# Six chunks of a fused 1x1 product by seven half-depth products instead of eight, in two gated layers, and a new order of small work in the last layer

## The chip, the cores and the metric

The kernel runs on one core of one Trainium2 chip. The metric is device time in microseconds (us). The engines are TensorE (PE, with its weight loads as PEld), VectorE (DVE), ScalarE (ACT), GpSimd (POOL) and SyncE (SP). SP and ACT also issue DMA transfers from their queues, and each engine works through a list of instructions of its own.

## The reference

Four layers act on one map of 512 channels and 64x64 pixels, each as `x = x + layer(group_norm(x))`, all in float32. Layer 0 is attention and isn't touched by the change. Layers 1 and 2 are the gated layers, and layer 3 is a linear attention:

```python
# layers 1 and 2: DIMS = [128, 256, 512]
fused = conv1x1(x, w_in, b_in)              # 512 -> 1024 channels
pwa, abc = fused[:, :128], fused[:, 128:]   # abc: 896 channels = 7 chunks of 128
dw_abc = dwconv7(abc, dw_w, dw_b)           # depthwise, 7x7
h = pwa * dw_abc[:, :128]
h = conv1x1(h, pw0_w, pw0_b) * dw_abc[:, 128:384]
h = conv1x1(h, pw1_w, pw1_b) * dw_abc[:, 384:]
return conv1x1(h, w_out, b_out)
...
# layer 3: 768 channels = 6 chunks
qkv0 = affine_nchw(conv2d(x, w_qkv), s_qkv, b_qkv)
agg = affine_nchw(conv2d(qkv0, w_dw, groups=768, pad=2), s_dw, b_dw)
...
```

## The kernel before

X stays on chip as 4 channel chunks of 128 partitions by 4096 pixels, cut into 8 blocks of 512 pixels. A "product" below is one matmul of a 128x128 weight with a 128x512 block. It is float32, and the profile shows each such product as two matmul records.

**Gated layers** (`_gated_convs`, twice). For each of the seven convolved chunks i and each block k, `fused(i, k)` makes four products (one for each input chunk) into one PSUM bank, and DVE moves the bank with the bias added into a plane buffer (L965). A DMA on ACT's queue then writes the plane to DRAM (tensor F[i], L720). There are two plane buffers, one for even and one for odd blocks. When all eight blocks of chunk i are there, `_PlaneConv.conv` does the depthwise convolution of the chunk as small matmuls: SP's queue loads the taps T (L729) and shifted rows S (L745), ACT copies S once more (L752), TensorE runs 8 parts of 96 records each into PSUM (`ps_cv`), DVE transposes the result (L806, and at the end four larger ones, L812), and ACT adds the bias (L1024).

Work of TensorE that needs no convolution is laid between the parts. `convolve(i, first, between)` issues the list `first` ahead of the first part and deals the list `between` out over the parts, by number of entries. The lists hold fused inputs, gates (`gate(i, b)`: products of earlier results, then a DVE multiply, L987) and outputs (`output`, products with `w_out`, then DVE additions into X, L999 and L1003). The order of TensorE's instructions is the program's. Those of DVE, ACT and the queues are laid out by a scheduler when the program is built. All products but the convolution's share four PSUM banks (pool `ps_mm`). Five weight buffers (`w2p`) and five large buffers (`hp`, one for each convolution result) rotate.

**Layer 3** (`_linear_attention`) already makes its fused product by `_Seven`: for a pair of weight chunks (a, b) and a pair of pixel blocks, with the depth of 512 halved, seven half-depth products (p1 to p7, two matmuls each) take the place of eight. It needs sums of the weights (`sums`, L844), differences of the blocks (`differences`, L858), two kept copies of PSUM banks made by ACT (L1225), two DVE additions to them (L891, L895), and four moves into planes (`put`: L1167 on ACT, L1172 and L1175 on DVE). Its weights are multiplied by `s_qkv` on POOL (L1125) and by the group norm's factor on ACT or DVE (`_Centered.scaled`, L363 and L366). `prepare(hf, q)` loads rows of k back and makes k positive (L1102), with its sums (L1335), ahead of the steps of a block.

The convolution and fill lists of the gated layers before the change are:

```python
b0, b12, b34, b56 = (inputs(c) for c in ((0,), (1, 2), (3, 4), (5, 6)))
...
convolve(0, b12[:6], b12[6:])
convolve(1, g[0][:3], g[0][3:] + b34[:6])
convolve(2, [], b34[6:])
convolve(3, b56[:4], b56[4:8] + g[1] + g[2])
convolve(4, [], b56[8:])
```

Of the kernel before, what the change touches and what calls it, by code (L numbers as in the profile page):

```python
# [127 lines left out]
def trunk_kernel(ctx: ExitStack, tc: tile.TileContext, a: dict, out: bass.AP):  # L128
# [42 lines left out]
    def new_stats():  # L171
# [11 lines left out]

    stats = _attention(tc, a, X, ident, gmask, neg2, small, new_stats, centered)

    late = ctx.enter_context(tc.tile_pool(name="late", bufs=1))
    s_qkv = late.tile([P, NQKV, P], FP, tag="s_qkv", name="s_qkv")
    nc.gpsimd.dma_start(
        out=s_qkv.rearrange("p i m -> p (i m)"),
        in_=bass.AP(a["L3_s"].tensor, a["L3_s"].offset, [[0, P], [1, NQKV * P]]),  # L190
    )
    stats = _gated_convs(tc, a, X, vcol, gmask, small, new_stats, centered, stats, F)
    _linear_attention(tc, a, X, vcol, vall, ident, gmask, small, centered, stats, F3, Z, s_qkv, out)


def _attention_general(tc, a, X, O, ident, neg2):
# [469 lines left out]
class _PlaneConv:  # L666
# [36 lines left out]
    def take(self, i, k, ps, fill):  # L703
# [18 lines left out]
            in_=t.rearrange("p n r w -> p n (r w)"),  # L722
        )

    def load(self, i, hf, wT, r):
        nc, f = self.nc, self.f
        nl = self.nl
# [96 lines left out]
class _Seven:  # L824
# [35 lines left out]
    def steps(self, a, b, s, t, x, bank, keep, put):  # L860

        nc = self.nc
        ps, kept = {}, {}

        def add(j, w, hs, first):

            if first:
                ps[j] = bank(j)  # L870
            for c in range(2):
                self.matmul(
                    ps[j], w[:, c], hs[c], start=(first and c == 0), stop=(c == 1),
                    skip_group_check=not first,
                )

        def p1():
            add(0, a[:, 0:2], [x(c, 0) for c in range(2)], True)
            kept[0] = keep(0, ps[0])

        def p5():
            add(1, s[0], t[0], True)
            kept[1] = keep(1, ps[1])

        def p2():
            add(0, a[:, 2:4], [x(2 + c, 0) for c in range(2)], False)
            put(0, 0, ps[0], None)

        def p7():
            add(2, s[2], t[2], True)  # L890
            nc.vector.tensor_add(kept[1], kept[1], ps[2])  # L891

        def p6():
            add(3, s[1], t[1], True)
            nc.vector.tensor_add(kept[0], kept[0], ps[3])  # L895

        def p3():
            add(1, s[3], [x(2 + c, 1) for c in range(2)], False)
            put(0, 1, ps[1], kept[0])
            put(1, 1, kept[1], kept[0])  # L900

        def p4():
            add(2, b[:, 2:4], t[3], False)
            put(1, 0, ps[2], kept[0])

        return [p1, p5, p2, p7, p6, p3, p4]


@with_exitstack
def _gated_convs(ctx, tc, a, X, vcol, gmask, small, new_stats, centered, stats, F):  # L910

# [2 lines left out]
    wp = ctx.enter_context(tc.tile_pool(name="cw", bufs=1))  # L916
    w2p = ctx.enter_context(tc.tile_pool(name="cw2", bufs=5))
    hp = ctx.enter_context(tc.tile_pool(name="ch", bufs=5))
    ps_mm = ctx.enter_context(tc.tile_pool(name="ps_mm", bufs=4, space=PSUM))
    ps_cv = ctx.enter_context(tc.tile_pool(name="ps_cv", bufs=4, space=PSUM))  # L920
    pc = _PlaneConv(ctx, tc, FORM, F, ps_cv, NL, 4, False)

    for layer in ("L1", "L2"):
# [24 lines left out]
        def product(w, hs):  # L948
# [2 lines left out]
                pc.matmul(ps, w(c), h, start=(c == 0), stop=(c == len(hs) - 1))  # L951
            return ps

        def taking(w, k):

            return product(lambda c: w[:, c, :], [pc.pixels(X[:, c, :], k) for c in range(NC)])

        def fused(i, k):
# [7 lines left out]
                    dst, src, vcol(pre + "b_in", 1 + i), None, ALU.add  # L966
                ),
            )
            if k == NB - 1 and len(w_in) < NDW:
                w_in.append(centered.scaled(weights("w_in", 1 + len(w_in)), rstd, nc.scalar))  # L970

        D = {}

        def gate(i, b):

# [13 lines left out]
        def output(chunks, b, o):  # L989
# [14 lines left out]
            if chunks[-1] == NDW - 1:  # L1004
                nc.vector.bn_stats(stats[:, o, b, :], xs)

        def blocks(f, i):
            return [lambda b=b: f(i, b) for b in range(NB)]

        def inputs(chunks):  # L1010
            return [lambda i=i, b=b: fused(i, b) for b in range(NB) for i in chunks]

        def outputs(*chunks):
            return [lambda b=b, o=o: output(chunks, b, o) for b in range(NB) for o in range(NC)]

        w_out = []

        def convolve(i, first, between):
# [6 lines left out]

            taps = a[f"{layer}_T"]
            pc.ahead(i, 0, taps)
            for f in first:
                f()

            parts = FORM.nr // FORM.run
            late = min(len(between) // 12, 2)
            early = len(between) - 3 * late
            done = 0
            for part, _ in enumerate(pc.conv(i, 0, taps, bias, D[i], True)):
                if part < parts:
                    upto = early * (part + 1) // parts
                else:
                    upto = done + late
                for f in between[done:upto]:  # L1040
                    f()
                done = upto

        b0, b12, b34, b56 = (inputs(c) for c in ((0,), (1, 2), (3, 4), (5, 6)))
        g = [blocks(gate, i) for i in range(NDW)]
        for f in b0:
            f()
        convolve(0, b12[:6], b12[6:])
        convolve(1, g[0][:3], g[0][3:] + b34[:6])
        convolve(2, [], b34[6:])  # L1050
        convolve(3, b56[:4], b56[4:8] + g[1] + g[2])
        convolve(4, [], b56[8:])
        convolve(5, g[3], outputs(3))
        convolve(6, [], g[4] + outputs(4))
        for f in g[5] + g[6] + outputs(5, 6):
            f()
    return stats


@with_exitstack  # L1060
def _linear_attention(ctx, tc, a, X, vcol, vall, ident, gmask, small, centered, stats, F, Z, s_qkv, out):

# [7 lines left out]
    vcs = 1.0 / N  # L1072

    lq = ctx.enter_context(tc.tile_pool(name="lq", bufs=1))
    w_proj = lq.tile([P, NC, C], FP, tag="w_proj", name="w_proj")
    nc.scalar.dma_start(out=w_proj, in_=a["L3_w_proj"])
    ksum = small.tile([P, NC, NB], FP, tag="ksum", name="ksum")
# [33 lines left out]
    with ExitStack() as st:  # L1111
# [8 lines left out]
        def weights(i):  # L1120
# [1 line left out]
                "p (c n) -> p c n", c=NC  # L1122
            )
            nc.sync.dma_start(out=t, in_=a["L3_w_qkv"][i])
            nc.gpsimd.tensor_tensor(  # L1125
                t, t, s_qkv[:, i].unsqueeze(1).to_broadcast([P, NC, P]), ALU.mult
            )
            return t

        w_qkv = [weights(i) for i in range(4)]  # L1130

# [21 lines left out]
            return ps  # L1153

        for i, w in enumerate(w_qkv):
            centered.scaled(w, rstd, nc.scalar if i else nc.vector)
        centered.began()

        def taken(k):
# [2 lines left out]

        def put(i, k, ps, more=None):

            if more is None:
                bias = vcol(pre + "b_qkv", i)
                pc.take(i, k, [ps], lambda d, x: nc.scalar.activation(d, x, AF.Identity, bias=bias))  # L1167
                return

            def fill(d, x, y):  # L1170
                if i % 2 == 0 or k % 2:
                    nc.vector.tensor_add(d, x, y)  # L1172
                    return
                for n in range(pc.pair):
                    nc.vector.scalar_tensor_tensor(  # L1175
                        d[:, n], x[:, n], step_b[:, i // 2 : i // 2 + 1], y[:, n],
                        ALU.add, ALU.add,
                    )

            pc.take(i, k, [ps, more], fill)  # L1180

        def fused(i, k):
            w = w_qkv[i]
# [71 lines left out]

        def more_weights():
            for i in (4, 5):
                w_qkv.append(centered.scaled(weights(i), rstd, nc.scalar))

        dve, pool = nc.vector, nc.gpsimd  # L1260
        made = [
# [159 lines left out]
        def steps(hf, q):  # L1421
# [7 lines left out]
            [  # L1429
                both(added, *early[:1]),  # L1430
                both(*early[1:4]),
                both(*early[4:7]),
                both(*early[7:10], prepare(0, 0)),
                both(*early[10:13]),
                both(*early[13:]),
            ],
# [200 lines left out]
```

## Time and profile before

| | |
|---|---|
| median of three runs | 3932.12 us (3929.24 to 3934.1) |
| the profiled execution's own time | 3927.94 us |
| its span in the trace | 3926.1 us |
| mean granted TensorE clock | 0.995 |
| matmul records on PE | 35622 |
| attention | to about 2290 us |
| layer 1 | about 2294 to 2801 us |
| layer 2 | about 2801 to 3307 us |
| layer 3 | about 3307 us to the end |

The profile lists each group of instructions with its line, engine, operation, the tile it writes and the tiles it reads, the shape, the number of instructions, then the busy time and the mean duration in ns, then the idle time of the engine ahead of the group and what ended it. Its windows give the busy time of each engine in a stretch of the span, its timelines give the instructions in order of time.

### The profile page before, as it was taken

What the parts mean: (1) busy time and instruction counts of PE and PEld (TensorE: products, weight loads), DVE (VectorE), ACT (ScalarE), POOL (GpSimd) and SP (SyncE); (2) the same over time, 40 slices, a digit from 0 to 9 for tenths busy, and PEclk for the clock granted to TensorE, in tenths of its full rate; (3) what the DMA queues carried; (4) which work ended last, traced back from release to release, by engine and by line L of the source; (5) the groups of instructions that cost most, each with busy time, mean ns of one, the idle gap of its engine ahead of it and who ended that gap; (6) DMA issues with size and microseconds to landing.
All of it is one profiled execution on the core that took longest, in us unless ns stands there. A gap on an engine that the chain in (4) does not pass through costs nothing. (4 is left out here: it accounts for less than half of the span.)

```text
span 3926.1 us, 81449 instructions
## 1 busy us (share of the span) xinstructions
PE 3847.3 (98%) x35622; PEld 1714.3 (44%) x35622; DVE 2370.2 (60%) x2607; ACT 1976.8 (50%) x2857; POOL 119.3 (3%) x101
## 2 busy tenths in 40 slices
PE   6999999999999999999999989999999999999999
PEld 4533335333354333453333335554455544455544
DVE  3577763777736777637767733466534576675435
ACT  3577762777726777536656644452244532354210
POOL 0000000000000000000000000000000000121110
PEclk9999999999999999999999999999999999999999
DMA  2000000000000000000000035552155520463334
GB/s 97 9 1 1 1 1 9 1 1 1 1 1 9 1 1 2 1 9 1 1 1 1 1 113 160 181 167 69 51 155 178 165 79 34 139 185 99 93 92 141
DMA packets 193943, 221.52 MB, mean 56 GB/s; under 512 B 13400, under 2 KB 138584, under 8 KB 193456
## 3 DMA queue, kind: packets, MB, share of 16 engines
q1 hardware_dynamic: 166832, 157.12, 14.3%
q10 hardware_dynamic: 26640, 58.72, 4.0%
q8 instruction: 281, 4.60, 0.5%
q14 instruction: 78, 0.64, 0.1%
q0 software_dynamic: 112, 0.45, 0.0%
HBM read 156.46 MB, written 59.77 MB: 55 GB/s over the span
## 5 line engine op out<-in xcount | busy, mean ns | idle before, releaser
L516 ACT ACTIVATE pt<-ps_s,A 128x512 f32<-128x512 f32 x2048 | 1286.2, 687 | 554.8 <-PE ps_s L508 527.0
L599 DVE TENSOR_TENSOR acc<-acc,pt 128x1024 f32<-128x1024 f32 x960 | 1175.6, 1225 | 331.7 <-ACT pt L516 306.1
L526 PE MATMUL av<-pt,V 64*64 64x512 f32 x8192 | 1112.5, 590 | 0.9 <-ACT pt L516 0.9
L508 PE MATMUL ps_s<-O,K 64*64 64x512 f32 x8192 | 1111.5, 589 | 0.0
L526 PEld LDWEIGHTS av<-pt,V 64*64 64x64 f32 x8192 | 339.7, 133 | 557.2 <-issue 525.4
L508 PEld LDWEIGHTS ps_s<-O,K 64*64 64x64 f32 x8192 | 334.3, 133 | 553.7 <-issue 308.6
L752 ACT COPY S<-S 32x1295 f32<-32x1295 f32 (+1 forms) x272 | 341.1, 1256 | 286.0 <-DMA S<-F 169.7
L693 PE MATMUL ps<-X,w_in_L 128*128 128x512 f32 x896 | 404.7, 604 | 5.2 <-DMA w_in_L<-in_L_w_in_dram 2.8
L965 DVE TENSOR_SCALAR plane<-ps,vec 128x512 f32<-128x512 f32 x112 | 83.7, 748 | 293.8 <-PE ps L693 245.8
L693 PEld LDWEIGHTS ps<-X,w_in_L 128*128 128x128 f32 x896 | 166.5, 191 | 204.0 <-issue 194.5
L693 PEld LDWEIGHTS ps_cv<-S,T 64*32 64x32 f32 x13824 | 194.0, 106 | 109.3 <-issue 73.7
L693 PE MATMUL ps_cv<-S,T 64*32 64x128 f32 x13824 | 231.5, 273 | 4.8 <-DVE turned L806 2.2
L463 PE MATMUL ps_qk<-X,wqkv 128*128 128x512 f32 x512 | 228.3, 599 | 2.8 <-ACT wqkv L363 2.8
L693 PE MATMUL ps<-h,w_out_L 128*128 128x512 f32 x512 | 228.4, 599 | 0.5 <-DVE X L999 0.5
L355 ACT ACTIVATE X<-X,gn_less 128x512 f32<-128x512 f32 x120 | 76.9, 710 | 218.1 <-DVE gn_less L102 206.1
L467 ACT ACTIVATE O<-ps_qk 128x512 f32<-128x512 f32 x32 | 19.1, 596 | 259.2 <-PE ps_qk L463 259.2
L1024 ACT ACTIVATE h<-h,vec 128x1024 f32<-128x1024 f32 x56 | 63.7, 1148 | 167.2 <-DVE h L812 167.0
L463 PEld LDWEIGHTS ps_qk<-X,wqkv 128*128 128x128 f32 x512 | 95.9, 192 | 114.3 <-issue 110.9
L693 PEld LDWEIGHTS ps<-h,w_out_L 128*128 128x128 f32 x512 | 94.3, 190 | 116.7 <-issue 100.5
L987 DVE SCALAR_TENSOR_TENSOR h<-ps,vec,h 128x512 f32<-128x512 f32 x112 | 82.5, 742 | 103.0 <-PE ps L693 97.5
L693 PE MATMUL ps<-h,pw_L 128*128 128x512 f32 x320 | 142.6, 598 | 0.7 <-DVE X L1003 0.7
L469 DVE TENSOR_SCALAR K<-ps_qk 128x512 f32<-128x512 f32 x32 | 22.1, 692 | 188.0 <-PE ps_qk L463 188.0
(155 smaller groups left out, 2783.3 us busy)
## 6 DMA issues: line engine op xcount, KB each, us to landing
T<-in_L_T_dram SPq DMA_DIRECT2D x112, 384.0 KB, 4.0
F<-plane ACTq DMA_DIRECT2D x112, 324.0 KB, 2.6
S<-F SPq DMA_DIRECT2D x224, 162.0 KB, 4.1
row<-G SPq DMA_DIRECT2D x80, 272.0 KB, 3.5
S<-G SPq DMA_DIRECT2D x96, 153.0 KB, 4.4
G<-plane ACTq DMA_DIRECT2D x48, 289.0 KB, 2.3
T<-in_L_T_dram SPq DMA_DIRECT2D x48, 256.0 KB, 3.7
out_dram<-y SPq DMA_DIRECT2D x32, 256.0 KB, 2.0
```

The lines of the kernel that those rows point to most:

```text
L355: self.nc.scalar.activation(xs, xs, AF.Identity, bias=less)
L463: nc.tensor.matmul(ps, w[:, n, c, :], X[:, c, cols], start=(c == 0), stop=(c == NC - 1))
L469: nc.vector.tensor_scalar(K[:, cols], ps, gain_in, None, ALU.mult)
L508: nc.tensor.matmul(ps[ts(half, D), ts(h, BLK)], K[rows, t * P + half * D : t * P + (half + 1) * D], QO[pair][rows, cols], start=True, stop ...
L516: nc.scalar.activation(pt[:, ts(h, BLK)], ps[:, ts(h, BLK)], AF.Exp, bias=A[:, t, h : h + 1])
L526: nc.tensor.matmul(av[half][rows, :], V[keys, t, rows], pt[keys, ts(h, BLK)], start=(t == 0), stop=(t == NT - 1),)
L599: nc.vector.tensor_add(acc, acc, pt)
L693: self.tc.keep_in_program_order(self.nc.tensor.matmul(*args, **kw))
L752: nc.scalar.copy(second, first)
L965: lambda dst, src: nc.vector.tensor_scalar(dst, src, vcol(pre + "b_in", 1 + i), None, ALU.add),
L987: nc.vector.scalar_tensor_tensor(d, ps, bias, d, ALU.add, ALU.mult)
L1024: nc.scalar.activation(t, t, AF.Identity, bias=vcol(pre + "dw_b", i))
```

## The change

Chunks 1 to 6 of both gated layers are made by `_Seven` in pairs of chunks (1,2), (3,4), (5,6) and pairs of blocks. Chunk 0 stays as it was. A group of seven steps of two matmuls takes the place of sixteen matmuls. The block differences live in one buffer of the pool `hp`, and those of the next group are made while a group runs, after its steps p2 and p3 and at its next start. `put` moves from layer 3 into `_PlaneConv` and serves both, and its last move (1, 1) goes from step p3 to step p4. `convolve` deals its list out by weights of the entries and not by their number, and the lists are cut anew. In layer 3 the load of `s_qkv` goes from POOL's queue ahead of the gated layers to ACT's queue at the start of layer 3. The factor `s_qkv` and the group norm's factor are applied in one DVE step for each 128x128 part. `prepare(0, 0)` comes one entry earlier in its list.

```diff
-    late = ctx.enter_context(tc.tile_pool(name="late", bufs=1))
-    s_qkv = late.tile([P, NQKV, P], FP, tag="s_qkv", name="s_qkv")
-    nc.gpsimd.dma_start(
...
+    def put(self, i, k, ps, more, bias, step):
+        nc = self.nc
+        if more is None:
+            self.take(i, k, [ps], lambda d, x: nc.scalar.activation(d, x, AF.Identity, bias=bias))
+            return
+        def fill(d, x, y):
+            if step is None:
+                nc.vector.tensor_add(d, x, y)
+                return
+            for n in range(self.pair):
+                nc.vector.scalar_tensor_tensor(
+                    d[:, n], x[:, n], step, y[:, n], ALU.add, ALU.add
+                )
+        self.take(i, k, [ps, more], fill)
...
         def p3():
             add(1, s[3], [x(2 + c, 1) for c in range(2)], False)
             put(0, 1, ps[1], kept[0])
-            put(1, 1, kept[1], kept[0])
 
         def p4():
             add(2, b[:, 2:4], t[3], False)
             put(1, 0, ps[2], kept[0])
+            put(1, 1, kept[1], kept[0])
...
+    keptp = ctx.enter_context(tc.tile_pool(name="ck", bufs=2))
...
-            if k == NB - 1 and len(w_in) < NDW:
+        diff = hp.tile([P, N], FP, tag="h", name="diff")
...
+        def more(n):
+            while len(w_in) < n:
                 w_in.append(centered.scaled(weights("w_in", 1 + len(w_in)), rstd, nc.scalar))
+        def summed(i):
+            t = [w2p.tile([P, NC, P], FP, tag="w", name="w_sum") for _ in range(2)]
+            t = [t[n // 2][:, n % 2 * 2 : n % 2 * 2 + 2] for n in range(4)]
+            wsum[i] = seven.sums(nc.vector, w_in[i], w_in[i + 1], t)
...
+        def keep(i, j, ps):
+            t = keptp.tile([P, BLK], FP, tag="kept", name="kept")
+            bias = step_b[:, (i + 1) // 2 : (i + 1) // 2 + 1] if j else vcol(pre + "b_in", 1 + i)
+            nc.scalar.activation(t, ps, AF.Identity, bias=bias)
+            return t
+        def put(i, k, ps, more):
+            short = i % 2 == 0 and k % 2 == 0
+            pc.put(
+                i, k, ps, more, vcol(pre + "b_in", 1 + i),
+                step_b[:, i // 2 : i // 2 + 1] if short else None,
+            )
+        def bank(j):
+            return ps_mm.tile([P, BLK], FP, tag="mm", name="ps7")
...
+        def group(i, k):
...
+            def step(n):
+                if n == 0:
+                    if i not in wsum:
+                        summed(i)
+                    steps.extend(seven.steps(...))
+                    for _ in mine:
+                        pass
+                steps[n]()
+                for _ in range({2: 2, 5: 4}.get(n, 0)):
+                    next(after, None)
+                if n == 6 and k == NB // 2 - 1:
+                    more(min(i + 4, NDW))
+            return [(0.5, lambda n=n: step(n)) for n in range(7)]
...
-            late = min(len(between) // 12, 2)
-            early = len(between) - 3 * late
+            total = sum(n for n, _ in between)
+            late = total / 12
...
-        convolve(0, b12[:6], b12[6:])
-        convolve(1, g[0][:3], g[0][3:] + b34[:6])
-        convolve(2, [], b34[6:])
-        convolve(3, b56[:4], b56[4:8] + g[1] + g[2])
-        convolve(4, [], b56[8:])
+        for b in range(NB):
+            fused(0, b)
+            if b == 2:
+                for _ in made[1, 0]:
+                    pass
+        convolve(0, b12[:10], b12[10:])
+        convolve(1, g[0][:3], g[0][3:] + b34[:12])
+        convolve(2, [], b34[12:])
+        convolve(3, g[1] + b56[:2], g[2] + b56[2:12])
+        convolve(4, [], b56[12:])
...
+    s_qkv = lq.tile([P, NQKV, P], FP, tag="s_qkv", name="s_qkv")
+    nc.scalar.dma_start(
...
-            nc.gpsimd.tensor_tensor(
-                t, t, s_qkv[:, i].unsqueeze(1).to_broadcast([P, NC, P]), ALU.mult
-            )
             return t
+        def scaled(i, w):
+            for c in range(NC):
+                nc.vector.scalar_tensor_tensor(
+                    w[:, c], w[:, c], rstd[:, c : c + 1], s_qkv[:, i], ALU.mult, ALU.mult
+                )
+            return w
...
         for i, w in enumerate(w_qkv):
-            centered.scaled(w, rstd, nc.scalar if i else nc.vector)
+            scaled(i, w)
...
-                w_qkv.append(centered.scaled(weights(i), rstd, nc.scalar))
+                w_qkv.append(scaled(i, weights(i)))
...
-                both(*early[4:7]),
-                both(*early[7:10], prepare(0, 0)),
+                both(*early[4:7], prepare(0, 0)),
+                both(*early[7:10]),
```

## The prediction

> **What bounds the kernel now.** I read the busy times first, then the windows around the gated layers' fused products, then the groups by shape, last the timelines where a convolution ends.
>
> ```profile
> PE 3847.3 (98%) x35622; PEld 1714.3 (44%) x35622; DVE 2370.2 (60%) x2607; ACT 1976.8 (50%) x2857; POOL 119.3 (3%) x101
> ```
> ```profile
> core 0: us, PE busy (x) PEld busy (x) DVE busy (x) ACT busy (x) POOL busy (x), PEclk, DMA share, GB/s
> 2334.00:2606.00 272.00, 272.00 (x4314) 139.55 (x4313) 110.81 (x129) 121.87 (x103) 0.00 (x0) 1.00 0.57 173
> 2606.00:2802.00 196.00, 193.26 (x1922) 92.35 (x1920) 139.20 (x193) 53.77 (x44) 0.00 (x0) 1.00 0.25 71
> 2839.00:3111.00 272.00, 271.43 (x4313) 139.23 (x4312) 110.01 (x128) 121.38 (x103) 0.00 (x0) 1.00 0.57 171
> ```
>
> In both stretches that hold chunks 1 to 6 (2334 to 2606 and 2839 to 3111) TensorE has no gap to speak of, DVE works 41% and ACT 45% of the time. So a product removed there is time removed, as long as the other engines keep up with what they are given instead.
>
> **The removed products.** A block of a chunk costs four products; in runs without a gap eight records (four products) take 3.43 us in the chain of waits, 0.857 each. Per layer three pairs of chunks by four pairs of blocks are 12 groups, each 14 matmuls instead of 16: 24 products less. 24 x 0.857 = **20.6 us per layer, 41.2 in both**; records fall by 96 to 35526.
>
> **What DVE and ACT get.** Layer 3 runs the same groups, so its rows price them:
>
> ```profile
> L965 DVE TENSOR_SCALAR plane<-ps,vec 128x512 f32<-128x512 f32 x112 | 83.7, 748 | 293.8 <-PE ps L693 245.8 <-DMA F<-plane 47.9
> L858 DVE TENSOR_TENSOR diff<-X,diff 128x512 f32<-128x512 f32 x16 | 10.5, 687 | 1.0 <-PE ps L693 0.6 <-ACT X L355 0.4
> L1225 ACT ACTIVATE kept<-ps,vec 128x512 f32<-128x512 f32 x11 | 7.5, 686 | 40.1 <-PE ps L693 34.3 <-DVE plane L1172 3.4 <-DMA G<-plane 2.3
> L1172 DVE TENSOR_TENSOR plane<-kept 128x512 f32<-128x512 f32 x11 | 9.8, 894 | 7.3 <-DMA G<-plane 7.3
> L1175 DVE SCALAR_TENSOR_TENSOR plane<-ps,step_b,kept 128x256 f32<-128x256 f32 x22 | 9.6, 476 | 3.6 <-PE ps L693 2.3 <-issue 1.3
> L895 DVE TENSOR_TENSOR kept<-kept,ps 128x512 f32<-128x512 f32 x11 | 7.5, 685 | 2.3 <-PE ps L693 2.0
> ```
>
> Per group on DVE: eight differences, 1.29 per adjacent pair in the timeline, 5.2 us; two additions to kept copies, 1.4; put (0,1) 0.7; put (1,1) 0.7 (its median); put (1,0) in four pieces of 128 columns. No row has that piece: a line through 476 ns at 256 columns and 742 at 512 (L987) gives 0.34, 1.4 for four; overlapped as pairs are (0.88 for two of L1175) about 1.3, which I take. Sum 9.3 us against 4 x 0.748 = 3.0 before: +6.3. Twelve groups 76, three weight sums of four 0.42 us steps 5: **DVE +81 us per layer**, 192 of 251 us, 76%. ACT: two kept copies and put (0,0), 2.1 us per group, 25 per layer: 147 of 251, 59%. Neither is the bound on average. The cover is thin where work bunches: TensorE needs 7 x 1.715 = 12.0 us for a group without a convolution part, DVE 9.3, and a convolution's end gives DVE two transposes (1.95 us) and four L812 (1.22 each), 6.8 us at once.
>
> ```profile
> 2502.09 20.87 PE L693 MATMUL ps<-X,w_in_L 128*128 128x512 f32 x48
> 2502.15 1.94 DVE L806 STREAM_TRANSPOSE h<-ps_cv 128x512 f32<-128x512 f32 x2 [0.72 <-PE ps_cv L693]
> 2504.12 3.50 DVE L812 STREAM_TRANSPOSE h<-h 128x1024 f32<-128x1024 f32 x3
> 2507.54 0.71 DVE L965 TENSOR_SCALAR plane<-ps,vec 128x512 f32<-128x512 f32 x1
> ```
>
> This is the end of convolution 2: the plane move is 2 us late, and nobody minds. Layer 3 shows what the same costs inside a group:
>
> ```profile
> 3397.18 3.77 DVE L815 STREAM_TRANSPOSE agg<-turned 128x512 f32<-128x512 f32 x4
> 3398.29 2.61 ACT L1291 ACTIVATE agg<-agg,beta,alpha 128x512 f32<-128x512 f32 x3 [8.04 <-DVE agg L815]
> 3400.81 0.80 DVE L1175 SCALAR_TENSOR_TENSOR plane<-ps,step_b,kept 128x256 f32<-128x256 f32 x2
> 3400.81 0.67 ACT L1225 ACTIVATE kept<-ps,vec 128x512 f32<-128x512 f32 x1
> 3401.53 3.78 PE L693 MATMUL ps<-X,w_qkv 128*128 128x512 f32 x4 [3.31 <-ACT kept L1225]
> 3405.10 2.93 PE L693 MATMUL ps<-diff,w_sum 128*128 128x512 f32 x4
> ```
>
> The kept copy stands on ACT behind activations that wait for DVE's transposes; step p2 waits 3.31 us for it.
>
> **Where TensorE will wait**, per layer, by following the changed program's instruction order on each engine with these durations:
>
> - *Layer start, +1.2.* Two differences of the first blocks stand on DVE ahead of the group norm's last multiply and of the first weight's scaling (L366). In layer 2 the chain goes 2804.92, 2805.13, 2805.32, product at 2806.16; two differences of 0.65 come between. Bounds 0 and 1.4.
> - *First two groups, +1.1.* They run back to back. On ACT, the plane DMA of put (1,1) waits for DVE and stands ahead of the next group's first kept copy. After p4 DVE does one difference, four pieces of put (1,0), one difference, put (1,1): 3.5 us; the copy ends about 4.4 us after p4, p2 is due at 3.4. Bounds 0 and 2.
> - *End of convolution 0, +0.5.* F[1] is now written by put (0,1) behind the transposes; then its DMA (2.5), the load of S (2.8 from issue at 2400.66 to first copy at 2403.43 now) and two ACT copies (2.5) end some 19.5 us after the last part, the next part is due at 20.6. A small backlog makes it late. Bounds 0 and 3.
> - *End of convolution 1, +2.0.* Group (3,0) passes into (3,1) without a part between. By adding up DVE's queue from the last part on, put (1,1) ends at 9.7 us, the kept copy behind its DMA at 10.5, p2 is due at 8.6. Bounds 0 and 3.3.
> - *End of convolution 2, +2.6.* Eight short gates (one product each) now follow group (3,3) at once. The third needs the bank that put (1,0) empties; DVE comes to it at 12.7 us, TensorE is there at 10.3. Bounds 0 and 3.3.
> - *Ends of convolutions 3 and 4, 0*: there a part or two-product gates follow, and DVE is ahead by the same count; up to 1 each.
>
> Sum +7.4, so a layer gains 20.6 - 7.4 = 13.2, **both 26.4 us**.
>
> **A rule against the change.** After the 3.31 us wait above, four records took 3.78 and 2.93 us instead of 1.72, another 3.3 us; a wait of 3.24 us at 3538.6 had no such tail. The Trainium skill, "TensorE: Matmul & The Clock Gate" (The HAM clock gate), says that the clock falls to half after an idle window of about 3.4 us and needs as long to come back, and warns of waits between groups that cycle through PSUM banks. By the rule my waits, all below 3.4, cost nothing more; by the row the two longest may cost 3.3 each per layer. I take 0 and put 2 x 3.3 into the range.
>
> **Edits with one answer.** The rationing by weight moves outputs around convolutions 5 and 6, where TensorE's idle time is 2.7 us per layer: 0, bounds ±1. Weight loads that end a pair stand on SP's queue ahead of S loads, and on DVE sums stand ahead of gates; by order their buffers come free in time (p2 of the last group): 0, if late up to 2. Removing POOL's 0.6 us issue of s_qkv in layer 1 frees no one.
>
> **Layer 3.** At its start the factor is ready at 3311.13. Before, POOL multiplied until 3312.3, then DVE scaled for 1.73 (beside POOL), first product at 3314.19. Now DVE does both in four pieces, 1.4 us: product at 3312.6, **-1.5**. Bounds: -2, or +1.5 if s_qkv's 0.39 MB, loaded only now on ACT's queue ahead of w_proj, lands late; w_proj itself is needed at 3491. Weights 4 and 5 are scaled on DVE, which waits for their DMA (landed 3362.4 and 3369.3) with a kept addition behind: 1.5 us late, its reader p4 two steps off, 0. put (1,1) in p4 comes where DVE already had it: 0. prepare(0,0) moves 3.3 us of DVE work (L1102, L1335) and two row loads on SP past one convolution part; the wait at 3538.6 hangs on the next block's rows: 0, bounds ±1.
>
> **Sum.** -26.4 - 1.5 = -27.9 on the profiled execution's 3927.94 (span 3926.1): 3900. That execution lies 4.2 below the median of 3932.12; on the median's footing 3904. I give 3903.
>
> **Rivals.**
> - *The cover is whole* (12%): the waits come out near 0, as in 2334 to 2606 now. -41.2 - 1.5: 3889. For it: averages of 76% and 59%; against: single in-order queues at convolution ends.
> - *DVE lags throughout* (9%): kept additions and puts fall behind in every convolution, 1.2 us per group x 24 = 29: -14, 3918. Layer 3 from 3314 to 3495 has PE idle 5.9 us in 11 groups, with the tail 9.2, 0.84 each, at a DVE share of 63%; here it is 76%. Against: more than half of the 9.2 is one place.
> - *Slower* (6%): ACT's kept copy is caught behind each convolution's end as at 3398, with the slow clock: 3.31 + 3.27 = 6.6 us. From seven such places (41.2/6.6 and layer 3's gain) the change loses; at the ends of convolutions 0 to 3 of both layers, 8 x 6.6 = 53: +10, 3942. Against it: in the changed order the first kept copy of the group at hand stands ahead of the bias activations at all these ends.
> - *Nothing in sum* (3%): half of that.
>
> The forecast has 70%; its own range is 3892 to 3914. With the rivals the range is 3888 to 3920. About 0.2% (7.9 us) is what a measurement of this kernel can tell from no change: faster 0.91, same 0.03, slower 0.06.
>
> **What would show it.** 35526 records on PE; in the two stretches DVE near 190 and ACT near 147 us in about 257; PE waits on ACT's kept copies and on DVE's puts of 5 to 9 us per layer, mostly at the ends of convolutions 1 and 2; first product of each gated layer 1.2 us later behind the group norm, that of layer 3 1.5 sooner. Wrong if the granted clock dips inside the stretches, or if convolution parts wait for S.

## The result, and the profile after

The changed kernel takes 3899.87 us (median of four runs, 3899.55 to 3903.08) against 3931.08 for the kernel before beside it: a ratio of 0.9922, 95% interval 0.9905 to 0.9939, or 31 us. The forecast was 3903. On another chip, later, it took 3904.14 (five runs, 3902.41 to 3906.8) against 3931.54, ratio 0.9929 (0.9915 to 0.9942). The profiled execution took 3899.94, its span is 3898.2.

From the page, the busy times, and from the windows the two stretches with chunks 1 to 6 (columns as before):

```profile
PE 3811.4 (98%) x35526; PEld 1692.3 (43%) x35526; DVE 2509.6 (64%) x2944; ACT 2017.3 (52%) x2909; POOL 109.3 (3%) x94
```
```profile
core 0: us, PE busy (x) PEld busy (x) DVE busy (x) ACT busy (x) POOL busy (x), PEclk, DMA share, GB/s
2334.00:2592.00 258.00, 254.12 (x4268) 130.25 (x4267) 177.41 (x273) 151.21 (x147) 0.00 (x0) 1.00 0.61 181
...
2826.00:3084.00 258.00, 254.88 (x4268) 130.53 (x4267) 177.64 (x275) 151.02 (x147) 0.00 (x0) 1.00 0.61 180
```

There are 96 records less, and each stretch is 14 us shorter (258 in place of 272). DVE goes from 41% to 69% and ACT from 45% to 59%. TensorE, with next to no gap before, now has 3 to 4 us of gaps, at the full clock.

Where the 27.9 us of span went is read from the start of each group norm's first product (gn_ps, L100) to the next one's:

| | before | after | difference |
|---|---|---|---|
| attention | 2295.24 | 2294.20 | -1.0 |
| layer 1 | 506.14 | 493.35 | -12.8 |
| layer 2 | 505.87 | 491.59 | -14.3 |
| layer 3, to the end of the span | 618.85 | 619.1 | +0.2 |

So in these two executions the whole gain lies in the gated layers, and layer 3 gained nothing. The changed kernel was profiled once more (changed_again below): there the gated layers are 10.7 and 13.5 us shorter than before and layer 3 is 3.6 longer, so a single pair of profiles tells a layer's gain to some 2 us in the gated layers and 3 in layer 3.

From one matmul record to the next product record 0.429 us pass when nothing waits; 48 records less per layer are the 20.6 us. What TensorE lost on top in the first profile (time from record to record less 0.429, and for the start the time from the group norm's first product), in us:

| place | predicted | layer 1 | layer 2 |
|---|---|---|---|
| start of the layer | 1.2 | 1.18 | 0.74 |
| slow clock behind the start | 0 | 0.53 | 0.32 |
| (1,0) to (1,1), first two groups | 1.1 | 1.28 | 1.15 |
| end of convolution 0 | 0.5 | 0 | 0 |
| end of convolution 1 | 2.0 | 1.27 | 1.26 |
| end of convolution 2 | 2.6 | 1.27 | 1.28 |
| end of convolution 3 | 0 | 1.18 | 0.26 |
| outputs at convolutions 5 and 6 | 0 | 0.34 | 0.34 |
| sum | 7.4 | 7.05 | 5.35 |

The rest to 20.6 less the measured gain (7.8 and 6.3) is under a microsecond per layer in many small pieces. In the row of convolution 2, 0.97 us lies at the gates right behind its end and 0.3 at two later gates. Two of these places in the timeline of the changed kernel; first, the second group of layer 1 (`put(0,1)`, its DMA, the DMAs of `put(1,0)` and `put(1,1)`, `put(1,1)` itself, the kept copy, the waiting product p2):

```profile
2341.57 0.69 DVE L729 TENSOR_TENSOR plane<-ps,kept 128x512 f32<-128x512 f32 x1 [0.27 <-PE ps L687]
...
2342.29 0.33 ACTq L714 DMA_DIRECT2D F<-plane  x1
...
2344.51 2.50 ACTq L714 DMA_DIRECT2D F<-plane  x2
...
2345.96 0.69 DVE L729 TENSOR_TENSOR plane<-kept 128x512 f32<-128x512 f32 x1 [0.89 <-DMA F<-plane]
...
2347.06 0.69 ACT L1017 ACTIVATE kept<-ps,vec 128x512 f32<-128x512 f32 x1 [1.55 <-PE ps L687]
...
2347.80 1.98 PE L687 MATMUL ps<-X,w_in_L 128*128 128x512 f32 x4 [1.12 <-ACT kept L1017]
```

The kept copy stands on ACT's queue behind the DMA of `put(1,1)`. The prediction had that. But DVE's own work is only a part of why `put(1,1)` is late: before it, DVE stood 0.89 us for the plane buffer, whose transfer had begun at 2342.29. Second, the end of convolution 2:

```profile
2498.97 2.74 PE L687 MATMUL ps<-h,pw_L 128*128 128x512 f32 x6
...
2501.05 1.08 DVE L732 SCALAR_TENSOR_TENSOR plane<-ps,step_b,kept 128x128 f32<-128x128 f32 x4
...
2502.28 3.15 PE L687 MATMUL ps<-h,pw_L 128*128 128x512 f32 x6 [0.57 <-DVE plane L732]
```

The fourth gate (in the prediction the third) waits for the bank that `put(1,0)` (L732) empties, for 0.57 us and not the 2.4 forecast.

### The profile page after: what moved, and what is told of

It is laid out like the page before. It is cut to its first block, busy times and chain, and to the rows that moved or that the text cites. A ratio compares the mean times of both kernels' runs of the same rounds, so it can differ in the third digit from the quotient of the medians.

```text
span 3898.2 us, 81595 instructions
## 1 busy us (share of the span) xinstructions
PE 3811.4 (98%) x35526; PEld 1692.3 (43%) x35526; DVE 2509.6 (64%) x2944; ACT 2017.3 (52%) x2909; POOL 109.3 (3%) x94
## 5 line engine op out<-in xcount | busy, mean ns | idle before, releaser
L687 PE MATMUL ps<-diff,w_sum 128*128 128x512 f32 x420 | 197.4, 602 | 0.5 <-issue 0.5
L687 PE MATMUL ps<-X,w_in_L 128*128 128x512 f32 x320 | 152.6, 617 | 12.9 <-ACT kept L1017 5.3
L819 DVE STREAM_TRANSPOSE h<-ps_cv 128x512 f32<-128x512 f32 x112 | 109.4, 1050 | 43.5 <-PE ps_cv L687 42.8
L468 PEld LDWEIGHTS ps_v<-wqkv,X 128*128 128x128 f32 x1024 | 119.4, 192 | 15.3 <-issue 15.3
```

Of the source, the lines that this page charges most:

```text
L468: nc.tensor.matmul(ps[:, ts(i, P)], X[:, c, ts(b * QT + i, P)], w[:, 2, c, :], start=(c == 0), stop=(c == NC - 1),)
L687: self.tc.keep_in_program_order(self.nc.tensor.matmul(*args, **kw))
L819: nc.vector.transpose(out, src)
```

## Experiments

All have the changed kernel as base. Layer lengths are taken as above. The runs plane3, plane_odd, pin_diff, diff_twice, diff_pool, pin_affine and l3_undone are one execution each. For scale: the changed kernel's nine executions took 3899.6 to 3906.8 us, and in the five profiles of kernels that are the same up to layer 3 (after, changed_again, pin_affine, l3_undone, prep_back) layer 1 lasted 493.2 to 495.5 and layer 2 491.6 to 493.4 us. A smaller difference shows nothing by itself.

**An extra plane, at the wrong place (plane3).** A plane buffer of its own was meant for the odd blocks of one chunk of a pair.

```diff
-                self.out[oy, ox] = t
+                self.out[oy, ox, 0] = self.out[oy, ox, 1] = t
+                if f.parts == 1 and len(self.out) > 2:
+                    t = sp.tile([P, self.pair, f.fh, f.fw], FP, tag="more", name="plane")
+                    nc.gpsimd.memset(t, 0.0)
+                    self.out[oy, ox, 1] = t
...
-        t = self.out[oy, ox]
+        t = self.out[oy, ox, i % 2]
```

> The changed kernel with one plane buffer more: in the gated layers the odd blocks of the two chunks of a pair get a plane of their own. My theory: where TensorE waits 1.28 and 1.15 us (layers 1 and 2) in front of the second group, the last move put(1,1) stood still for the plane's transfer that put(0,1) had begun 3.7 us before, and so does the wait behind convolution 3 (1.18 and 0.26 us). With its own plane those four waits go: -3.9 us in the two layers. Those behind convolutions 1 and 2 (1.27 and about 1.3 us in each layer) have a full DVE queue behind them and stay. Rival (the prediction's own reason): DVE's queue of 3.5 us holds put(1,1) everywhere; then nothing changes, within 1 us.

3900.21 us. The first-group waits were 0.95 and 0.92, that behind convolution 3 in layer 1 1.41, layers 493.7 and 492.5: nothing gained. The condition picks the second plane, which is that of the even blocks, so the run says nothing of the theory; plane_odd below repeats it.

**An extra plane for the odd blocks (plane_odd).** As above, with another condition and a name for the buffer's tag:

```diff
-                if f.parts == 1 and len(self.out) > 2:
+                if f.parts == 1 and ox < 0:
```

> The changed kernel; here the odd blocks of the two chunks of a pair have a plane buffer each (the run plane3 gave the extra buffer to the even blocks, so it left this open). put(1,1) no longer waits for the plane's transfer that put(0,1) began, and DVE gets to it earlier everywhere. Theory: the waits in front of the second group (1.28 and 1.15 us in layers 1 and 2) and behind convolution 3 (1.18 and 0.26 us) go, that behind convolution 1 (1.27 in each) at least halves: -4 to -6 us in the two layers. Rival (DVE's own queue of some 3.5 us holds the move, whatever the plane does): at most -1 us.

3898.91 us; layers 491.7 and 489.7, -1.6 and -1.9, just short of the -4 to -6 expected for both. The timeline of this run at the same place as above:

```profile
2342.65 0.68 DVE L733 TENSOR_TENSOR plane<-kept 128x512 f32<-128x512 f32 x1
...
2346.63 0.69 ACT L1021 ACTIVATE kept<-ps,vec 128x512 f32<-128x512 f32 x1
...
2347.95 1.88 PE L691 MATMUL ps<-X,w_in_L 128*128 128x512 f32 x4
```

`put(1,1)` now runs before `put(0,1)`, the kept copy is ready in time and the product has no wait. The waits of the first groups and of the end of convolution 1 are gone in both layers, those behind convolution 2 unchanged (0.74 + 0.23). So the buffer that the two chunks of a pair share set two of the three places in question, but not in one way. At the first groups DVE stood for the transfer, 0.89 us. Behind convolution 1 it did not: the changed kernel, then plane_odd, by DVE's timeline:

```profile
2447.26 0.71 DVE L729 TENSOR_TENSOR plane<-ps,kept 128x512 f32<-128x512 f32 x1
...
2449.02 1.10 DVE L732 SCALAR_TENSOR_TENSOR plane<-ps,step_b,kept 128x128 f32<-128x128 f32 x4
...
2450.62 0.70 DVE L729 TENSOR_TENSOR plane<-kept 128x512 f32<-128x512 f32 x1
```
```profile
2447.09 0.72 DVE L733 TENSOR_TENSOR plane<-ps,kept 128x512 f32<-128x512 f32 x1
...
2447.69 0.71 DVE L733 TENSOR_TENSOR plane<-kept 128x512 f32<-128x512 f32 x1
```

In the changed kernel DVE comes to `put(1,1)` without a pause, from a transpose, the four pieces of `put(1,0)` and a difference. With the second buffer the scheduler lays it ahead of them. So there the work on DVE ahead of the move holds it, and the buffer takes the wait away by changing the order; the run does not separate the two. How long the transfer holds DVE differs between executions: in changed_again it held `put(1,1)` for 5.31 us in the middle of convolution 0 of layer 1, where TensorE then lost 1.1 us and the first profile has no wait:

```profile
2364.58 0.69 DVE L729 TENSOR_TENSOR plane<-kept 128x512 f32<-128x512 f32 x1 [5.31 <-DMA F<-plane]
```

The wait behind convolution 3 stayed (2.14 in layer 1): there the kept copy stands behind a copy of S that waits for its load. By the timeline of plane_odd:

```profile
2542.16 1.27 ACT L769 COPY S<-S 32x1295 f32<-32x1295 f32 x1 [1.78 <-DMA S<-F]
...
2544.19 1.99 PE L691 MATMUL ps<-X,w_in_L 128*128 128x512 f32 x4 [1.98 <-ACT kept L1021]
```

Layer 3 took 620.5 in this run, so only 1 us of 3.5 shows in the total.

**The first differences held back (pin_diff).**

```diff
-                for _ in made[1, 0]:
-                    pass
+                for d in made[1, 0]:
+                    tc.keep_in_program_order(d)
```

> The changed kernel with the eight block differences of the first group held on DVE behind the third plane move of a gated layer, so that none stands ahead of the group norm's last multiply and of the first weight's scaling. Theory: the first product comes 5.8 us after the group norm's first product in layer 1 and 4.8 in layer 2, as before the change (with the change 7.00 and 5.52): -1.9 us in the two layers together. Rival: the start hangs on something else (weights, POOL's and ACT's centering) and stays at 7.0 and 5.5.

3896.26 us; the first product comes 5.82 and 4.78 us after the group norm's first, as expected. DVE at the start of layer 2, changed kernel:

```profile
2790.96 0.68 DVE L871 TENSOR_TENSOR diff<-X 128x512 f32<-128x512 f32 x1
2791.56 0.15 DVE L123 TENSOR_TENSOR gn_r<-gn_r,gn_t 128x4 f32<-128x4 f32 x1
2791.64 0.68 DVE L871 TENSOR_TENSOR diff<-X 128x512 f32<-128x512 f32 x1
2792.24 0.68 DVE L360 TENSOR_TENSOR w_in_L<-w_in_L,gn_r 128x512 f32<-128x512 f32 x1
```

and with the differences held back:

```profile
2791.15 0.16 DVE L123 TENSOR_TENSOR gn_r<-gn_r,gn_t 128x4 f32<-128x4 f32 x1
2791.35 0.69 DVE L360 TENSOR_TENSOR w_in_L<-w_in_L,gn_r 128x512 f32<-128x512 f32 x1
```

So the two differences were in the way; they cost 1.18 us in layer 1 and 0.74 in layer 2, where 1.2 was forecast for each. Layer 1 became 1.25 us shorter (492.1), layer 2 stayed (491.6): it lost the gain again at the end of convolution 3 (1.31 in place of 0.26). Of the total's 3.7 us most is layer 3 (615.6), which the edit doesn't touch.

**Differences made twice on DVE (diff_twice).**

```diff
+            once = seven.differences(nc.vector, view(k), diff)
+            again = seven.differences(nc.vector, view(k), diff)
+            for a in once:
+                next(again)
+                yield a
```

> The changed kernel, but every block difference of the gated layers is made twice on DVE: 96 more differences of 0.65 us per layer, 62 us, which brings DVE from about 200 to about 262 us in a stretch of 258. My theory (the cover holds on the average and fails where work bunches, so it is nearly used up): TensorE waits for DVE in most groups, 15 to 30 us per layer, 30 to 60 us in all. Rival (the cover is ample, the waits come from transfers and order): under 8 us in all.

3953.74 us, +54, as expected: layers 519.3 and 518.0, 26 us more in each. In its window DVE is at 81%, and the clock has dips:

```profile
2334.00:2615.00 281.00, 260.11 (x4263) 131.88 (x4262) 227.03 (x358) 148.81 (x146) 0.00 (x0) 0.97 0.57 166
```
```profile
2460.09 3.78 PE L687 MATMUL ps<-X,w_in_L 128*128 128x512 f32 x4 [3.65 <-ACT kept L1021]
...
2517.37 7.55 PE L687 MATMUL ps<-h,pw_L 128*128 128x512 f32 x10 [3.70 <-DVE plane L732]
```

The second fence is its timeline. The waits behind convolutions 1 and 2 have grown to 3.65 and 3.70, and the records behind them run at half speed (four in 3.78, ten in 7.55 us, where 0.429 each is usual). A wait of 1.1 us costs 1.1; grown to 3.7, with the slow records behind it, it cost 6.5 and 7.0. Behind convolution 3 of layer 1 TensorE even stood 5.94 us. So the cover that DVE's free time gives at 69% is thin: 57 us more of busy time on DVE per layer cost 26.

**Differences on POOL (diff_pool).**

```diff
-            return seven.differences(nc.vector, view(k), diff)
+            return seven.differences(nc.gpsimd, view(k), diff)
```

> The changed kernel with the block differences of the gated layers on POOL in place of DVE: DVE falls by 66 us per layer. My theory of the waits alone: with DVE at half load those behind convolutions 1 and 2 and the start of a layer go, 3 to 4 us per layer, -7 us in all. Rival: a POOL difference takes 1.26 us in layer 3, ten us for a group of 12, and DVE beside POOL took 1.73 us for a multiply of 128x512 at the old start of layer 3 where such a shape else takes 0.68; then the differences are late in groups that run back to back and DVE's own moves stretch: slower by 5 to 30 us. I hold the rival likelier.

3908.54 us, +8.6, the rival: layers 497.2 and 495.5. The waits behind convolution 2 are gone, as the theory had it; but those of the first groups and of convolution 1 doubled (2.4 each), and the start, which the theory had go, came later still: the first product stands 7.56 and 6.65 us behind the group norm's, for 7.00 and 5.52. The timeline at the first groups shows `put(1,1)` drawn out to 1.77 us beside a POOL difference:

```profile
2346.59 2.98 POOL L871 TENSOR_TENSOR diff<-X 128x512 f32<-128x512 f32 x2 [0.89 <-PE ps L687]
2346.66 1.77 DVE L729 TENSOR_TENSOR plane<-kept 128x512 f32<-128x512 f32 x1 [1.56 <-DMA F<-plane]
```

**Activations of layer 3 behind the kept copies (pin_affine).** `keep_in_program_order` holds an instruction behind those that stand before it in the program on its engine.

```diff
-                    lambda: nc.scalar.activation(
+                    lambda: tc.keep_in_program_order(nc.scalar.activation(
...
```

> The changed kernel with the affine activations of layer 3's convolution results held on ACT behind the kept copies that stand before them in the program. My theory of layer 3's longest wait (4.53 us at 3372.61, and the next eight records 3.78 and 2.63 us in place of 2 x 1.72): the kept copy stands on ACT behind activations that wait for DVE's transposes, and the slow records are the clock's answer to the wait. Both go: -4.5 - 3.0 = -7.5 us in layer 3, and the granted clock has no dip there. Rivals: the kept copy is late in itself, because DVE's late plane move stops the group (then at most -1 us); or the slow records have another cause (then -4.5 us, and they stay).

3908.25 us, +8.3 where -7.5 was expected. First the place in the changed kernel:

```profile
3366.08 0.93 DVE L729 TENSOR_TENSOR plane<-kept 128x512 f32<-128x512 f32 x1 [3.81 <-DMA G<-plane]
...
3368.27 3.76 DVE L828 STREAM_TRANSPOSE agg<-turned 128x512 f32<-128x512 f32 x4
3369.37 2.61 ACT L1388 ACTIVATE agg<-agg,beta,alpha 128x512 f32<-128x512 f32 x3 [7.81 <-DMA S<-G]
...
3372.61 3.78 PE L687 MATMUL ps<-X,w_qkv 128*128 128x512 f32 x4 [4.53 <-ACT kept L1322]
```

then in this run:

```profile
3373.45 1.20 ACT L765 COPY S<-S 32x1207 f32<-32x1207 f32 x1 [8.01 <-DVE turned L819]
3374.67 0.69 ACT L1322 ACTIVATE kept<-ps,vec 128x512 f32<-128x512 f32 x1
3375.41 3.39 PE L687 MATMUL ps<-X,w_qkv 128*128 128x512 f32 x4 [2.27 <-ACT kept L1322]
```

The activations are out of the way, but the next in ACT's queue, a copy of S, stood ahead of the kept copy, TensorE waited 2.27 us, and DVE again stood 3.73 us for the plane's transfer. What the place gained was lost at later ones: layer 3 took 622.3, 3.2 more than in the changed kernel's first profile and as much as in its second (622.4), and the other 5 us lie in stages that the edit doesn't touch. So the run doesn't show that the edit slows the kernel; it shows no gain. The theory that the kept copy needs only the activations out of its way fell with this run.

**Layer 3's own edits.** l3_undone takes back the scaling (POOL and then DVE or ACT) and the place of `prepare(0, 0)`, but not that of the load of `s_qkv`; prep_back takes back that place alone:

```diff
-                both(*early[4:7], prepare(0, 0)),
-                both(*early[7:10]),
+                both(*early[4:7]),
+                both(*early[7:10], prepare(0, 0)),
```

> The changed kernel with layer 3's own edits taken back: POOL multiplies the weights by s_qkv and DVE or ACT scales them by the group norm's factor, and the rows of k are prepared one list entry later (the load of s_qkv stays where the change put it, since there is no room for it before). Theory: the first product of layer 3 comes 6.9 us after the group norm's first one in place of 4.3; of these 2.6 us up to 1 is given back because the clock is slow there anyway, so layer 3 lasts 1.5 to 2.6 us longer than the 616.7 to 619.7 us of the four runs with these edits. Rival: the late order costs as much as the start gains, and layer 3 lasts 617 to 619.5 us as in the kernel before (618.85).

> The changed kernel itself, once more, on the same chip as the next two: 3899 to 3902 us.

> The changed kernel with the preparation of the first rows of k in layer 3 back in its old list entry and nothing else. Theory: the wait of TensorE for the transposes into turned, 200 to 206 us into layer 3, with 1.5 to 2.5 us from one product to the next, shows in all eight profiles with the early entry and in neither of the two with the old one; it goes: 1 to 2 us less in layer 3 (a slow stretch of the clock less would be 1.7 more), so 3897 to 3899 us. The wait of 3.9 or 5.1 us some 93 us into the layer is not touched by this edit. Rival: l3_undone was short by chance, or by its scaling on POOL; then 3899 to 3902.

l3_undone took 3896.51, with the first product 5.6 us behind the group norm's and layer 3 the shortest of all, 613.55: both sides of the expectation missed. DVE's scaling took 0.69 us there and 1.73 in the kernel before, so taking POOL's multiply back gave up only 1.3 of the 2.6 us at the start. changed_again took 3904.14, above its range; its layers were 495.5, 492.3 and 622.4, so the same kernel moves by some 4 us. prep_back took 3900.75 (3897.93 to 3906.18) beside it, above the 3897 to 3899 expected and within the rival's range; that is 3.4 less than changed_again, with runs that overlap, and its layer 3 lasted 618.2. To see through that spread, layer 3 is cut at TensorE's convolution records, whose number is the same in all (us, worked out from the traces):

```
                 group norm to   records    records       records
                 first product   1 to 257   1281 to 1537  1537 to 1793   layer 3
before                6.94        27.97        14.97         24.63        618.9
after                 4.32        28.89        17.60         26.53        619.1
changed_again         4.56        28.98        17.90         27.42        622.4
plane3                4.32        28.17        16.75         24.28        616.7
pin_diff              4.51        25.17        16.76         27.50        615.6
pin_affine            4.31        25.82        19.49         26.04        622.3
l3_undone             5.62        25.17        14.95         26.20        613.6
prep_back             4.36        28.65        14.97         26.54        618.2
best                  4.31        28.98        14.98         26.24        621.2
best_pool             5.84        28.84        14.97         23.68        614.9
```

The third column of numbers follows one edit alone: 14.95 to 14.98 in all five kernels with `prepare(0, 0)` in its old place, 16.75 to 19.49 in those with the early one (the runs not listed: 16.83 to 18.17). The early place costs 1.8 to 4.5 us in this stretch. What of it reaches the end isn't settled: among the changed kernel and its variants, layer 3 lasts 615.6 to 622.4 us with the early place and 613.6 to 621.2 with the old one, since other stretches move as much. The second column holds the wait for the kept copy some 93 us into the layer; it is 25.17 in the two kernels where no slow records followed that wait. Timeline of the changed kernel, then of prep_back:

```profile
3478.81 1.06 DVE L1206 TENSOR_SCALAR k<-row 128x256 f32<-128x256 f32 x4
...
3482.42 1.87 DVE L1432 TENSOR_REDUCE ksum<-agg 128x1 f32<-128x512 f32 x3
...
3484.21 1.31 DVE L819 STREAM_TRANSPOSE turned<-ps_cv 128x512 f32<-128x512 f32 x2
...
3484.97 1.98 PE L687 MATMUL ps<-agg,w_proj 128*128 128x512 f32 x4 [0.89 <-DVE turned L819]
```
```profile
3480.58 5.66 PE L687 MATMUL ps<-agg,w_proj 128*128 128x512 f32 x12
...
3483.48 1.31 DVE L819 STREAM_TRANSPOSE turned<-ps_cv 128x512 f32<-128x512 f32 x2
```

DVE makes k positive and sums it while a convolution part ends; the transposes that free the bank come late. In prep_back the twelve products run through.

**Versions put together.** both is plane_odd with pin_diff; best adds prep_back; best_pool adds the old scaling to that.

> The runs plane_odd and pin_diff in one kernel. Theory: -6 to -8 us against the changed kernel's 3899.9, so 3892 to 3894. Rival (the waits are set by DVE's queue): 3897 to 3900.

> The runs plane_odd, pin_diff and prep_back in one kernel. Theory: their parts add up, as they lie in different places: the gated layers at 489.1 and 488.5 us as in the run both (changed kernel 493.35 and 491.59), layer 3 at 613 to 619; 3892 to 3896 us, and in every case faster than the changed kernel by 4 us or more. Rival: what is gained in the gated layers is given back in layer 3 by slow stretches of the clock, as in the profile of both (layer 3 at 621.6): 3897 to 3900.

> The run best with the scaling of layer 3's weights taken back too (POOL by s_qkv, then DVE or ACT), so that layer 3 is the one of l3_undone behind the faster gated layers. Open is why l3_undone had the shortest layer 3 (613.55 us). Theory, chance: the wait of TensorE for the kept copy 93 us into the layer comes as 3.9 or 5.1 us, with or without slow records, in kernels that are the same there; layer 3 then lasts 616 to 621 us here and the time is 3895 to 3900 us. Rival, the scaling: with POOL's scaling the work of the first 90 us is laid out otherwise and the wait is 3.9 us without slow records again; layer 3 lasts 612 to 615 us, and the time is 3889 to 3894.

both: 3896.08 (four runs, 3894.1 to 3898.41), ratio 0.9911 (0.9894 to 0.9927), between the theory's range and the rival's. best: 3898.05 (3888.28 to 3899.3), ratio 0.9907 (0.9892 to 0.9922), on the chip where the changed kernel took 3904.14; no run of the one overlaps the other. It gained the 4 us or more that were expected, but its time lies in the rival's range, with layer 3 at 621.2. best_pool: 3894.92 (3888.51 to 3901.25), ratio 0.9908 (0.9894 to 0.9921). The program of the gated layers is the same in all three; they lasted 489.1 and 488.5 in both, 491.0 and 490.0 in best, 493.9 and 488.9 in best_pool. Against the changed kernel's first profile that is 7.3, 4.0 and 2.1 us less in the two layers, of the 12.4 that the listed waits cost. In layer 1 of best_pool more than half of what is missing against both lies behind convolution 3, at a wait that none of the edits touches, with records at half speed behind it:

```profile
2544.10 3.42 PE L691 MATMUL ps<-X,w_in_L 128*128 128x512 f32 x4 [2.18 <-ACT kept L1021]
```

For best_pool neither side came true: the wait in layer 3 was the long one with slow records (28.84), and layer 3 still lasted only 614.9. It has l3_undone's total by other places. Whether the scaling on POOL helps layer 3, or chance did it twice, stays open.

## Why the prediction was right

- *Removed products, 20.6 us per layer.* Right: 48 records less in each, 0.429 apart.
- *DVE +81, ACT +25.* ACT's was right: +24 in each layer. DVE's was too high: +71 in each layer, and 177 us in the stretch where 192 were forecast. The conclusion, not the bound but thin where work bunches, was tested by diff_twice; diff_pool, which frees DVE, also slows its moves and so is no clean test of the other side.
- *Waits of 7.4 us per layer.* 7.05 and 5.35, by the listed places. The start was right in cause (pin_diff) and in size for layer 1. The first groups were right in size, but not wholly in cause: on top of its own work DVE stood 0.89 us for the plane's transfer, which the prediction left out. The ends of convolutions 1 and 2 came to 1.27 for 2.0 and 1.28 for 2.6. There the cause, DVE's list, fits the timelines; it was got through sooner than by adding up durations, as adjacent instructions overlap. End of convolution 0: nothing in the first profile. End of convolution 3: up to 1.2 there, just over the bound of 1, and 1.9 in changed_again; its cause, a copy of S ahead of the kept copy, was not named. Net, 13.2 was forecast; 12.8 and 14.3 were measured, and 10.7 and 13.5 in changed_again.
- *The clock rule.* Taking 0 inside the stretches was right for the changed kernel: no wait there is above 1.3 us in the first profile (1.76 in changed_again), and the clock is 1.00. But a wait below 3.4 us is not safe, as the rule in the prediction had it: best_pool has half speed behind 2.18 us at the same kind of place, and diff_twice behind 3.65 and 3.70. Behind the starts, where it is slow anyway, a later first product costs 0.5 and 0.3 more, which the sum lacked.
- *Layer 3, -1.5.* It came to +0.2, and two terms were wrong. The start was taken as four scaling pieces, 1.4 us, ahead of the first product; the product begins after the first piece, so it stands 2.6 us sooner:

```profile
3282.84 1.14 DVE L1233 SCALAR_TENSOR_TENSOR w_qkv<-w_qkv,gn_r,s_qkv 128x128 f32<-128x128 f32 x4
3283.45 17.12 PE L687 MATMUL ps<-X,w_qkv 128*128 128x512 f32 x33 [2.09 <-DVE w_qkv L1233]
```

  `prepare(0, 0)` was put at 0, with bounds of 1 on either side; it costs 1.8 to 4.5 in its stretch, outside them. Only the wait for the next rows was looked at, not the transposes queued behind the moved work on DVE. The two errors hid each other in part.
- *The total.* The forecast of 3903 lies 3.1 us above the first chip's median and 1.1 below the second's. That 27.9 us of span was forecast for the profiled execution and 27.9 measured is luck: the gated layers gave 0.7 more than forecast, layer 3 1.7 less, and 1 us is the attention, which was not touched. In changed_again the span is only 21.0 us shorter than that of the kernel before.
- *Rivals.* A whole cover (3889) would have needed no waits. A lag throughout (3918) would look like diff_twice. The slower case needed the kept copy caught with the slow clock at eight ends; the longest wait at a convolution's end in the two profiles, 1.76 us of idle time in changed_again, is half of the 3.31 that it assumed, and no slow record followed it.

## What to carry to other kernels

Cheaper arithmetic on the bound engine pays in full less the waits at a few seams, and these can be listed beforehand by following each in-order queue there; ask of each move not only what its engine does, but whether the buffer it writes is still being transferred, and whether a second buffer would let the scheduler lay it earlier. Place every moved step against what stands behind it on its engine, and not only against its own reader. Where an execution moves by 4 us, judge an edit by the stretch that it touches, cut at the same records in all traces.

## What the runs showed of the hardware

- The same wait of TensorE, 3.31 us for the kept copy in layer 3, was followed by the slow clock in two executions and not in two others. In pin_diff and in plane3, by the timeline of TensorE:

```profile
3370.67 1.98 PE L687 MATMUL ps<-X,w_qkv 128*128 128x512 f32 x4 [3.32 <-ACT kept L1322]
3372.49 1.88 PE L687 MATMUL ps<-diff,w_sum 128*128 128x512 f32 x4
```
```profile
3373.81 3.78 PE L691 MATMUL ps<-X,w_qkv 128*128 128x512 f32 x4 [3.31 <-ACT kept L1326]
3377.39 3.13 PE L691 MATMUL ps<-diff,w_sum 128*128 128x512 f32 x4
```

  The other two are the kernel before, where it was slow as well, and l3_undone, where it was not. In diff_pool even a wait of 2.28 us had four records of 2.73 or 3.40 us behind it, in both layers, while 2.21 had none; in best_pool 2.18 had four of 3.42. In all fourteen traces the slow stretches that begin and end inside the span last 3.41 us or two, three or four times that. The Trainium skill, "TensorE: Matmul & The Clock Gate" (The HAM clock gate), has the clock fall after an idle window of about 3.4 us, and says that the window runs freely. That fits the chance in it and the lengths of the slow stretches, but the runs show the slow clock after waits well below that length.
- TensorE can count as busy and still lose the clock: 32 products of one column each (128x1) are followed by records at half speed, and the granted clock of the next 3.4 us is 0.50 (timeline and window of the changed kernel). In all fourteen traces a slow stretch of 3.41 us begins within 1.1 us of the start of the last of the 32; no run was made without them:

```profile
3462.77 3.73 PE L687 MATMUL ps_pb<-vec,w_proj 128*128 128x1 f32 x32
3466.36 3.66 PE L687 MATMUL ps<-agg,w_proj 128*128 128x512 f32 x4
```
```profile
3466.40:3469.80 3.40, 3.40 (x5) 1.06 (x5) 0.48 (x3) 0.00 (x0) 0.00 (x0) 0.50 0.98 251
```

- POOL slows DVE only in part. In diff_pool DVE's additions with both sources in SBUF (L729 from kept alone) rose from 699 to 934 ns on average, those that read PSUM as well stayed at 689 (691 before). The Trainium skill, "GPSIMD Engine Reference" (Specifications), says as much: DVE meets POOL when it has two SBUF inputs.
